# A two-layer graph network: the nodes between the layers as a pipeline of chunks, with shared message buffers

## The chip, the cores and the metric

The kernel runs on one core of a Trainium2 chip. The core has five engines, each with an instruction queue of its own that is worked off in order: TensorE (PE in the profile; its weight loads are listed apart as PEld), VectorE (DVE), ScalarE (ACT), GpSimd (POOL) and SyncE (SP), which here only starts DMA transfers. Engines wait for each other by semaphores. The metric is the time of one execution on the device in microseconds. The tables quote single records of a profiled execution, which is one more execution beside the timed ones.

## What is computed

There are 6250 nodes with 64 features and 206,250 edges, sorted by destination. Each of two layers normalizes the nodes, sends a message along every edge, sums the messages at their destinations, and adds an update to the nodes. Cut to what matters:

```
h  = relu(layernorm(x))                       # over the 64 features
m  = segment_sum(relu(h[src] + ea16 @ We.T + be), dst)
g  = batchnorm((h + m) @ W1.T + b1)           # over the nodes
x  = x + relu(g) @ W2.T + b2                  # end of layer 0
h  = relu(layernorm(x))
y  = relu(concat(h[src], ea64) @ Mw.T + Mb)
z  = segment_sum(y, dst)
x  = x + relu(concat(h, z) @ Uw.T + Ub)       # end of layer 1
```

The change concerns the two lines in the middle: from `relu(g)` to the normalized `h` of layer 1 and to `h @ Mw_h.T + Mb`, the part of the message that depends on the source node alone, which the kernel keeps as a table with one row per node.

## The kernel before

Nodes lie in 49 tiles of 128, and the middle part works on chunks of 8 tiles: six full ones and one of a single tile. Edges come in groups of 16 x 128.

Edges are summed in two ways. The first 71 groups are sorted on the chip. For each group VectorE works out a place for every edge (`rank`), PE and ScalarE make the edge's row (`rows`), and GpSimd writes the rows to memory with 16 indirect DMAs (`scatter`, L605). A block of sorted rows then belongs to one tile of 128 destinations. There are 35 such blocks, of seven chunks each (`chunk`): a one-hot matrix of sources picks rows of the table by matmul (`gp`, L319), the message is finished (L324, or L326 and L327), a one-hot matrix of destinations is built (`hot_d`, L329), and a matmul sums the messages into `pa` (L333). The loading of a block (`eb`) and the preparation of its columns run ahead of it (`prepare`, `sources`).

The last 30 groups are not sorted. GpSimd fetches their rows of the table with 16 indirect DMAs per group (`gather`, L384) into `gat`, which has four buffers. `direct` then handles a group in two halves of 8 x 128 edges: the part from the edge features on PE (L402), its sum with the gathered rows on VectorE (L406), the relu on ScalarE (L407), a one-hot matrix on VectorE (L410) and the matmul into `pd` (L415), which is added to `acc` (L417). In the kernel before, `direct` has message and one-hot buffers of its own, `msg_d` and `hot_g`, two of each.

`unsorted` ties the two ways together in each layer. It issues the gathers of a group, lets the sorted stream advance by 4 steps (layer 0) or 8 (layer 1), a step being a chunk, and then calls `direct` for the group of three turns earlier.

After layer 0's sums come, on VectorE and PE, a few operations that find out whether any edge was left over (L727 to L733, the result is `any_i`); `general` loops over such edges, zero times for these inputs, and the engines load its number of rounds from `any_i`. Then batch norm is finished from statistics per tile (L757 to L768) and applied with a relu in seven parts of 896 columns (L771).

The middle is the loop from L780 on. For each chunk: product with W2 (`py`, L784); x loaded and b2 added (L786, L787); the sum (L788), stored as x1 (L789) for the end of layer 1; `norm_relu`, which is mean, centering, square, variance, root, reciprocal and the scaled maximum (L217 to L228); `transposed` in two halves through one PSUM bank (L240, L241); the product with the message weight (`pt`, L795); the bias (L797); the store of the table (L799); and `split` (L249 to L252), which keeps the table on the chip as three bf16 parts for the one-hot matmuls of layer 1. GpSimd's gathers of layer 1 wait until the table is stored.

The order in each queue comes from a scheduler that takes the program's order and the buffers of its pools into account: an instruction that writes a buffer waits until the readers of its former contents are done. Only where the program asks for it is an order kept as written.

Of the kernel before, what the change touches and what calls it, by code (L numbers as in the profile page):

```python
# [49 lines left out]
NB = 49  # L50
NP = P * NB
# [44 lines left out]
def gnn_kernel(  # L96
# [22 lines left out]
    nc = tc.nc  # L119

    const = ctx.enter_context(tc.tile_pool(name="const", bufs=1))
# [5 lines left out]
    def bank(shape, name, tag, bufs=1, dtype=F32):  # L127
        return ps.tile(shape, dtype, name=name, tag=tag, bufs=bufs)
# [103 lines left out]
    def by_node(t):  # L232
        return t[:, :NP].rearrange("c (j p) -> c j p", j=NB)
# [162 lines left out]
    def direct(layer, g, gat, ea, to, pool):  # L396

        pd = bank([P, P], "pd", "rk")
        for a in range(0, GT, 8):
            pm = bank([P, 8, D], "pm_d", "pm", 2)  # L400
            if layer == 0:
                nc.tensor.matmul(pm, ea[:, a // 8, :], we0, start=True, stop=True)  # L402
# [3 lines left out]
            nc.vector.tensor_add(msg, pm, gat[:, a:a + 8, :])  # L406
# [76 lines left out]
    with tc.tile_pool(name="sort", bufs=1) as sort:  # L483
# [177 lines left out]
        for j0, j1 in chunks:  # L661
            n = j1 - j0
# [27 lines left out]
    for g in range(GS, NG):  # L690
# [4 lines left out]
    nc.vector.scalar_tensor_tensor(marked[:, GS * GT:], dst_d, float(PAD), wide,  # L695
                                   op0=OP.is_lt, op1=OP.mult)

    def unsorted(layer, table, steps, per_group, window_of, done):
# [28 lines left out]
    most = ln.tile([P, 1], F32, name="most")  # L727
    nc.vector.tensor_reduce(most, marked, AX.X, OP.max)
    p = bank([P, P], "most_p", "tr")
    nc.tensor.transpose(p, most.to_broadcast([P, P]), ident)  # L730
    any_f = ln.tile([1, 1], F32, name="any_f")
    nc.vector.tensor_reduce(any_f, p[0:1, :], AX.X, OP.max)
    nc.vector.tensor_scalar(any_i, any_f, float(NB), None, op0=OP.mult)  # L733

    w2_sb = weight(w2_t, "w2_sb")
    mx_sb = weight(mw_t[0:D, :], "mx_sb")
    uh_sb = weight(uw_t[0:D, :], "uh_sb")
    uz_sb = stacked(uw_t[D:2 * D, :], "uz_sb")
    b2_b = spread(b2, "b2_b")
    mb_b = spread(mb, "mb_b")  # L740
    ub_b = spread(ub, "ub_b")
    gamma_c = column(gamma, "gamma_c")
    beta_c = column(beta, "beta_c")
# [32 lines left out]
    late = ctx.enter_context(tc.tile_pool(name="late", bufs=1))  # L776
    h1t = late.tile([D, NP], F32, name="h1t")
    x1 = dram.tile([NP, D], F32, name="x1")
    x1_rows = x1.rearrange("(j p) d -> p j d", p=P)
    for j0, j1 in chunks:  # L780
        n = j1 - j0
        py = bank([P, 8, D], "py", "gp", 2)
        for j in range(j0, j1):
            nc.tensor.matmul(py[:, j - j0, :], by_node(acc)[:D, j, :], w2_sb, start=True, stop=True)  # L784
        xs = ln.tile([P, 8, D], F32, name="xc", bufs=2)[:, :n, :]
        nc.sync.dma_start(xs, x_rows[:, j0:j1, :])  # L786
        nc.vector.tensor_add(xs, xs, b2_b[:, None, :].to_broadcast([P, n, D]))  # L787
        nc.vector.tensor_add(xs, xs, py[:, :n, :])  # L788
        nc.sync.dma_start(x1_rows[:, j0:j1, :], xs)  # L789
        h = ln.tile([P, 8, D], F32, name="h", bufs=2)  # L790
        norm_relu(h, xs)
        transposed(h1t, h, j0, j1)
        pt = bank([P, 8, D], "pt", "gp", 2)
        for j in range(j0, j1):
            nc.tensor.matmul(pt[:, j - j0, :], by_node(h1t)[:, j, :], mx_sb, start=True, stop=True)  # L795
        tabf = ln.tile([P, 8, D], F32, name="tabf", bufs=2)
        nc.vector.tensor_add(tabf[:, :n, :], pt[:, :n, :],  # L797
                             mb_b[:, None, :].to_broadcast([P, n, D]))
        nc.sync.dma_start(table1_rows[:, j0:j1, :], tabf[:, :n, :])  # L799
        split(tabf, j0, j1)  # L800


    def output(h_t, z_t, x_b, to, pool):
# [97 lines left out]
```

## Time and profile before

| What | us |
|---|---|
| Median of three runs (lowest, highest) | 3044.73 (3044.18, 3052.03) |
| The profiled execution, and its span | 4316.56, 4314.7 |
| PE busy, PEld busy, DVE, ACT, POOL (whole span) | 2107.8, 1511.2, 1591.5, 622.3, 2089.7 |
| Last scatter, first gather of layer 0 | 2117.4, 2120.91 |
| Batch norm finished (start of the first relu, L771) | 2990.65 |
| First product of the middle (L784) | 2991.84 |
| First message of layer 1 (L326), first gather of layer 1 | 3088.90, 3089.98 |
| One scatter, one gather (L605, L384), mean | 1.035, 0.944 |

How to read it: each engine's busy time is an average over stages that have different limits, so the stages are read one by one. A line of the timeline or of the groups has the start, the duration, the engine, the source line, the operation with its output and inputs, the shape, and in brackets how long the engine had been idle before it and what released it. "Issue" and "remote" name idle time for which the profile shows no releaser on this core. The profiled execution is 1.42 times as long as the median.

### The profile page before, as it was taken

What the parts mean: (1) busy time and instruction counts of PE and PEld (TensorE: products, weight loads), DVE (VectorE), ACT (ScalarE), POOL (GpSimd) and SP (SyncE); (2) the same over time, 40 slices, a digit from 0 to 9 for tenths busy, and PEclk for the clock granted to TensorE, in tenths of its full rate; (3) what the DMA queues carried; (4) which work ended last, traced back from release to release, by engine and by line L of the source; (5) the groups of instructions that cost most, each with busy time, mean ns of one, the idle gap of its engine ahead of it and who ended that gap; (6) DMA issues with size and microseconds to landing.
All of it is one profiled execution on the core that took longest, in us unless ns stands there. A gap on an engine that the chain in (4) does not pass through costs nothing.

```text
span 4314.7 us, 58769 instructions
## 1 busy us (share of the span) xinstructions
PE 2107.8 (49%) x22799; PEld 1511.2 (35%) x22799; DVE 1591.5 (37%) x3467; ACT 622.3 (14%) x1313; POOL 2089.7 (48%) x2106
## 2 busy tenths in 40 slices
PE   3344554544455544545335332234456665566666
PEld 2233332333333323333123111113444454445545
DVE  7333443443344333434113111113244453444445
ACT  2111111111111111111011000001111111111111
POOL 6556555555655555565642665552233433443341
PEclk6666766766677667667568555555577776777777
DMA  8564655645555555655232111112144443444442
GB/s 204 147 186 158 185 146 155 192 144 171 180 169 169 156 137 155 188 178 146 75 121 79 28 28 25 25 26 72 43 145 137 142 145 127 134 139 131 160 136 80
DMA packets 310816, 556.78 MB, mean 129 GB/s; under 512 B 100484, under 2 KB 174468, under 8 KB 301572
## 3 DMA queue, kind: packets, MB, share of 16 engines
q1 hardware_dynamic: 231744, 470.66, 35.6%
q0 software_dynamic: 67072, 79.29, 7.3%
q10 hardware_dynamic: 11716, 3.03, 0.4%
q8 instruction: 181, 2.97, 0.3%
q14 instruction: 103, 0.84, 0.1%
HBM read 367.38 MB, written 185.38 MB: 128 GB/s over the span
## 4 chain that ended last, share of the span: by engine, by line
PE 35%; another core or an unknown queue 32%; issue 18%; DMA 6%; DVE 4%; ACT 3%; POOL 1%; SPq 0%; DVEq 0%; ACTq 0%; POOLq 0%
PE pa L333 11%; PE gp L319 8%; PE gp L267 5%; DMA eb<-place 3%; PE pm L258 3%; PE pd L415 3%; DMA gat<-table,src_d 1%; PE pm_d L258 1%; PE pm_d L402 1%; DVE msg L326 1%; ACT msg L324 1%; DMA xc<-in_x 1%; POOL gat L384 1%; PE at_p L265 1%
## 5 line engine op out<-in xcount | busy, mean ns | idle before, releaser
L605 POOL DMA_INDIRECT place<-to,ix x1136 | 1175.7, 1035 | 935.6 <-ACT at L266 467.6
L384 POOL DMA_INDIRECT gat<-table,src_d x960 | 906.0, 944 | 1077.3 <-DVE msg_d L406 759.6
L333 PE MATMUL pa<-hot_d,msg 128*64 128x128 f32 x7000 | 623.7, 316 | 794.6 <-issue 419.3
L333 PEld LDWEIGHTS pa<-hot_d,msg 128*64 128x64 f32 x7000 | 467.2, 157 | 999.4 <-issue 490.9
L329 DVE TENSOR_TENSOR hot_d<-cbank,dl 128x1024 f32<-128x1024 f32 (+1 forms) x490 | 539.4, 1104 | 693.9 <-remote 405.2
L319 PE MATMUL gp<-tab,hot_s 128*128 128x64 bf16 x5250 | 263.2, 209 | 276.7 <-issue 239.4
L319 PE MATMUL gp<-tab,st 128*128 128x64 bf16 x5250 | 259.6, 203 | 248.8 <-issue 160.1
L267 PE MATMUL gp<-we,at 128*128 128x512 f32 (+1 forms) x490 | 306.2, 709 | 89.2 <-issue 59.6
L324 ACT ACTIVATE msg<-gp 128x512 f32<-128x512 f32 (+1 forms) x245 | 135.1, 551 | 1408.6 <-remote 854.9
L319 PEld LDWEIGHTS <-hot_s 128*128 128x128 bf16 x5250 | 215.8, 108 | 340.9 <-issue 296.5
L310 DVE TENSOR_SCALAR hot_s<-st,pcol 128x1024 bf16<-128x1024 bf16 (+1 forms) x245 | 111.9, 461 | 579.1 <-remote 444.3
L319 PEld LDWEIGHTS <-st 128*128 128x128 bf16 x5250 | 214.4, 105 | 307.2 <-issue 301.3
L326 DVE TENSOR_TENSOR msg<-gp,eb 128x512 f32<-128x512 f32 (+1 forms) x245 | 152.2, 628 | 370.5 <-remote 253.3
L327 ACT ACTIVATE msg<-msg 128x512 f32<-128x512 f32 (+1 forms) x245 | 142.4, 584 | 881.2 <-DVE msg L326 729.5
L415 PE MATMUL pd<-hot_g,msg_d 128*64 128x128 f32 x1920 | 199.5, 348 | 121.9 <-DVE acc L417 68.1
L402 PE MATMUL pm_d<-we,ea_d 128*128 128x512 f32 x120 | 104.1, 965 | 273.6 <-DVE msg_d L406 174.0
L415 PEld LDWEIGHTS pd<-hot_g,msg_d 128*64 128x64 f32 x1920 | 152.0, 177 | 210.4 <-issue 189.2
L258 PE MATMUL pm<-we,ea 128*128 128x128 f32 x1136 | 193.4, 314 | 66.0 <-DMA ea<-in_ea 25.5
L417 DVE TENSOR_TENSOR acc<-acc,pd 128x128 f32<-128x128 f32 x60 | 17.2, 287 | 494.7 <-remote 387.0
L258 PEld LDWEIGHTS pm<-we,ea 128*128 128x128 f32 x1136 | 165.1, 218 | 90.2 <-issue 60.8
L410 DVE TENSOR_TENSOR hot_g<-cbank,rel_d 128x1024 f32<-128x1024 f32 x120 | 145.3, 1216 | 116.4 <-remote 65.2
L407 ACT ACTIVATE msg_d<-msg_d 128x512 f32<-128x512 f32 x120 | 75.4, 629 | 524.2 <-DVE msg_d L406 381.5
(133 smaller groups left out, 1843.2 us busy)
## 6 DMA issues: line engine op xcount, KB each, us to landing
eb<-place SPq DMA_DIRECT2D x70, 2050.0 KB
place<-minus SPq DMA_DIRECT2D x35, 2050.0 KB
st<-src_rows SPq DMA_DIRECT2D x210, 256.0 KB
hots<-hot_s SPq DMA_DIRECT2D x210, 256.0 KB
st<-hots SPq DMA_DIRECT2D x210, 256.0 KB
ea<-in_ea SPq DMA_DIRECT2D x71, 512.0 KB
place<-to,ix POOLq DMA_INDIRECT x1136
gat<-table,src_d POOLq DMA_INDIRECT x960
```

The source lines that it names most:

```text
L258: nc.tensor.matmul(half_tiles[:, 2 * k:2 * k + 2, :], ea[:, k, :], we1, start=True, stop=True)
L267: nc.tensor.matmul(gp[:, :n, :], at[:n * ED, :], we0[:n * ED, :n, :], start=True, stop=stop)
L319: nc.tensor.matmul(gp[:, t, :], hot_s[:, t, :], tab[:, sb, k, :], start=(layer == 1 and k == 0), stop=(k == 2 and (layer == 1 or t == n - 1)))
L324: nc.scalar.activation(msg[:, :n, :], gp[:, :n, :], AF.Relu)
L326: nc.vector.tensor_add(msg[:, :n, :], gp[:, :n, :], eb[:, a:b, 0:D])
L329: nc.vector.tensor_tensor(hot_d[:, :n, :], slot_p[:, None, :].to_broadcast([P, n, P]), dl[:, a:b, :].to_broadcast([P, n, P]), op=OP.is_equal)
L333: nc.tensor.matmul(pa[at:at + D, :], msg[:, t, :], hot_d[:, t, :], start=(a + t < 2), stop=(a + t >= T - 2))
L384: nc.gpsimd.indirect_dma_start(out=gat[:, t, :], out_offset=None, in_=table, in_offset=bass.IndirectOffsetOnAxis(ap=src_d[:, k:k + 1], axi ...
L402: nc.tensor.matmul(pm, ea[:, a // 8, :], we0, start=True, stop=True)
L410: nc.vector.tensor_tensor(hot, slot_p[:, None, :].to_broadcast([P, 8, P]), rel_d[:, k:k + 8, None].to_broadcast([P, 8, P]), op=OP.is_equal)
L415: nc.tensor.matmul(pd[at:at + D, :], msg[:, t, :], hot[:, t, :], start=(a + t < 2), stop=(a + t >= GT - 2))
L605: i = nc.gpsimd.indirect_dma_start(out=place[:, :], out_offset=bass.IndirectOffsetOnAxis(ap=ix[:, t:t + 1], axis=0), in_=to[:, t, :], in_o ...
```

## The change

Four things change.

1. `direct` takes its two buffers from the same rings as the sorted chunks (`msg` and `hot_d`, two buffers each) instead of having `msg_d` and `hot_g`.
2. The operations that make `any_i` and the loads of the later weights move from behind layer 0's gathers to ahead of them. So does a new preparation: `xc`, which is x + b2 with its mean over the features taken away, for all nodes; and `w2cw`, a pair of weights: W2 with the mean of its columns taken away, and W2 itself.
3. In the middle, a chunk is multiplied with both weights. Since the mean over features is linear, the product with the centered weight plus `xc` is already the centered node (`cen`), without a mean to be found first. The plain node (product with W2 itself, plus x + b2) is needed for the end of layer 1 alone; ScalarE copies the product out of PSUM and GpSimd adds it.
4. The chunks run as a pipeline that is written out: each turn issues the stages of several chunks (relu of the next, linear of this one, normalization of the one before, the message product of the one before that, and so on), and PE, VectorE and ScalarE keep this order.

```diff
             else:
                 edge_terms_1(pm, ea[:, a // 2:a // 2 + 4, :])
-            msg = pool.tile([P, 8, D], F32, name="msg_d", bufs=2)
+            msg = work.tile([P, 8, D], F32, name="msg")
             nc.vector.tensor_add(msg, pm, gat[:, a:a + 8, :])
             nc.scalar.activation(msg, msg, AF.Relu)
-            hot = pool.tile([P, 8, P], F32, name="hot_g", bufs=2)
+            hot = work.tile([P, 8, P], F32, name="hot_d")
...
+    most = ln.tile([P, 1], F32, name="most")
...
+    nc.vector.tensor_scalar(any_i, any_f, float(NB), None, op0=OP.mult)
...
+    w2cw = const.tile([D, 2, D], F32, name="w2cw")
+    nc.scalar.dma_start(w2cw[:, 1, :], w2_t)
+    w2m = ln.tile([D, 1], F32, name="w2m")
+    nc.vector.tensor_reduce(w2m, w2cw[:, 1, :], AX.X, OP.add)
+    nc.vector.tensor_scalar_mul(w2m, w2m, 1.0 / D)
+    nc.vector.tensor_scalar(w2cw[:, 0, :], w2cw[:, 1, :], w2m, None, op0=OP.subtract)
+    late = ctx.enter_context(tc.tile_pool(name="late", bufs=1))
+    mid_stack = ExitStack()
+    mid = mid_stack.enter_context(tc.tile_pool(name="mid", bufs=1))
+    xc = mid.tile([P, NB, D], F32, name="xc")
+    for j0, j1 in chunks:
+        n = j1 - j0
+        nc.sync.dma_start(xc[:, j0:j1, :], x_rows[:, j0:j1, :])
+        nc.vector.tensor_add(xc[:, j0:j1, :], xc[:, j0:j1, :], b2_b[:, None, :].to_broadcast([P, n, D]))
+        mean = ln.tile([P, 8, 1], F32, name="mean")
+        nc.vector.tensor_reduce(mean[:, :n, 0], xc[:, j0:j1, :], AX.X, OP.add)
+        nc.vector.tensor_scalar_mul(mean[:, :n, :], mean[:, :n, :], 1.0 / D)
+        nc.vector.tensor_sub(xc[:, j0:j1, :], xc[:, j0:j1, :], mean[:, :n, :].to_broadcast([P, n, D]))
...
-    for a in range(0, NP, NP // 7):
-        b = a + NP // 7
-        nc.scalar.activation(acc[:D, a:b], acc[:D, a:b], AF.Relu, bias=bn_shift, scale=bn_scale)
...
-    for j0, j1 in chunks:
-        n = j1 - j0
-        py = bank([P, 8, D], "py", "gp", 2)
...
+    class Nodes:
...
+        def relu(self):
+            t = acc[:D, self.j0 * P:self.j1 * P]
+            nc.scalar.activation(t, t, AF.Relu, bias=bn_shift, scale=bn_scale)
+
+        def linear(self):
+            self.pc = bank([P, 8, D], "pc", "gp", 2)
+            self.py = bank([P, 8, D], "py", "pm", 2)
+            for k, to in enumerate((self.pc, self.py)):
+                for j in range(self.j0, self.j1):
+                    nc.tensor.matmul(to[:, j - self.j0, :], by_node(acc)[:D, j, :], w2cw[:, k, :],
+                                     start=True, stop=True)
+
+        def centered(self):
+            n = self.n
+            self.cen = mid_2.tile([P, 8, D], F32, name="cen", bufs=2)[:, :n, :]
+            nc.vector.tensor_add(self.cen, self.pc[:, :n, :], xc[:, self.j, :])
+            self.sq = ln.tile([P, 8, D], F32, name="sq")[:, :n, :]
+            nc.scalar.activation(self.sq, self.cen, AF.Square)
+            xs = ln.tile([P, 8, D], F32, name="xc", bufs=2)[:, :n, :]
+            nc.sync.dma_start(xs, x_rows[:, self.j, :])
+            nc.gpsimd.tensor_add(xs, xs, b2_b[:, None, :].to_broadcast([P, n, D]))
+            y = mid_2.tile([P, 8, D], F32, name="y", bufs=2)[:, :n, :]
+            nc.scalar.copy(y, self.py[:, :n, :])
+            nc.gpsimd.tensor_add(xs, xs, y)
+            nc.sync.dma_start(x1_rows[:, self.j, :], xs)
+
+        def variance(self):
+            self.var = mid_2.tile([P, 8, 1], F32, name="var", bufs=2)[:, :self.n, :]
+            nc.vector.tensor_reduce(self.var[:, :, 0], self.sq, AX.X, OP.add)
+            nc.scalar.activation(self.var, self.var, AF.Sqrt, bias=eps, scale=1.0 / D)
+
+        def norm(self):
+            n = self.n
+            rstd = ln.tile([P, 8, 1], F32, name="rstd")
+            nc.vector.reciprocal(rstd[:, :n, :], self.var)
+            h = ln.tile([P, 8, D], F32, name="h", bufs=2)
+            nc.vector.scalar_tensor_tensor(h[:, :n, :], self.cen, 0.0,
+                                           rstd[:, :n, :].to_broadcast([P, n, D]),
+                                           op0=OP.max, op1=OP.mult)
+            transposed(h1t, h, self.j0, self.j1)
+
+        def product(self):
+            self.pt = bank([P, 8, D], "pt", ("pa", "rk")[self.c % 2])
+            for j in range(self.j0, self.j1):
+                nc.tensor.matmul(self.pt[:, j - self.j0, :], by_node(h1t)[:, j, :], mx_sb,
+                                 start=True, stop=True)
...
+    step = ((-1, Nodes.relu), (2, Nodes.product), (3, Nodes.second), (0, Nodes.linear),
+            (2, Nodes.table), (1, Nodes.variance), (3, Nodes.third), (0, Nodes.centered), (1, Nodes.norm))
+    with tc.manual_schedule(engines={mybir.EngineType.PE, mybir.EngineType.DVE,
+                                     mybir.EngineType.Activation}):
+        for k in range(-1, len(nodes) + 3):
+            for far, stage in step:
+                if 0 <= k - far < len(nodes):
+                    stage(nodes[k - far])
```

`table`, `second` and `third`, left out here, are the bias with the store of the table, and the two halves of `split`. GpSimd's adds and the DMAs of SP are not among the engines whose order is kept: the scheduler places them. In the changed kernel two of GpSimd's adds of b2 (L826) come to stand among the scatters of layer 0, behind the 48th and the 112th, because they need nothing but x and b2.

More of the change, by code (lines that the diff above doesn't have):

```diff
@@ L696, in gnn_kernel @@
                                    op0=OP.is_lt, op1=OP.mult)
+    most = ln.tile([P, 1], F32, name="most")
+    nc.vector.tensor_reduce(most, marked, AX.X, OP.max)
+    p = bank([P, P], "most_p", "tr")
+    nc.tensor.transpose(p, most.to_broadcast([P, P]), ident)
+    any_f = ln.tile([1, 1], F32, name="any_f")
+    nc.vector.tensor_reduce(any_f, p[0:1, :], AX.X, OP.max)
+    nc.vector.tensor_scalar(any_i, any_f, float(NB), None, op0=OP.mult)
+    mx_sb = weight(mw_t[0:D, :], "mx_sb")
+    uh_sb = weight(uw_t[0:D, :], "uh_sb")
+    uz_sb = stacked(uw_t[D:2 * D, :], "uz_sb")
+    b2_b = spread(b2, "b2_b")
+    mb_b = spread(mb, "mb_b")
+    ub_b = spread(ub, "ub_b")
+    gamma_c = column(gamma, "gamma_c")
+    beta_c = column(beta, "beta_c")
+    w2cw = const.tile([D, 2, D], F32, name="w2cw")
[16 more added lines that the diff above has]
+        nc.vector.tensor_sub(xc[:, j0:j1, :], xc[:, j0:j1, :], mean[:, :n, :].to_broadcast([P, n, D]))
     def unsorted(layer, table, steps, per_group, window_of, done):
@@ L724, in gnn_kernel @@
              lambda d: finish_0(d, None))
[L727 to L743, printed above, removed]
     def more_0(b, delta, pool):
@@ L768, in gnn_kernel @@
     nc.vector.tensor_sub(bn_shift, beta_c, bn_shift)
-    for a in range(0, NP, NP // 7):
-        b = a + NP // 7
-        nc.scalar.activation(acc[:D, a:b], acc[:D, a:b], AF.Relu, bias=bn_shift, scale=bn_scale)
     table1 = dram.tile([NP, D], F32, name="table1")
     table1_rows = table1.rearrange("(j p) d -> p j d", p=P)
-    late = ctx.enter_context(tc.tile_pool(name="late", bufs=1))
     h1t = late.tile([D, NP], F32, name="h1t")
@@ L779, in gnn_kernel, with __init__, table, second @@
     x1_rows = x1.rearrange("(j p) d -> p j d", p=P)
-    for j0, j1 in chunks:
-        n = j1 - j0
-        py = bank([P, 8, D], "py", "gp", 2)
[L783 to L800, printed above, removed]
+    class Nodes:
+        def __init__(self, c):
+            self.c = c
+            self.j0, self.j1 = chunks[c]
+            self.n = self.j1 - self.j0
+            self.j = slice(self.j0, self.j1)
+        def relu(self):
[39 more added lines that the diff above has]
+                                 start=True, stop=True)
+        def table(self):
+            n = self.n
+            self.tabf = ln.tile([P, 8, D], F32, name="tabf", bufs=2)[:, :n, :]
+            nc.vector.tensor_add(self.tabf, self.pt[:, :n, :], mb_b[:, None, :].to_broadcast([P, n, D]))
+            nc.sync.dma_start(table1_rows[:, self.j, :], self.tabf)
+            nc.scalar.copy(tab[:, self.j, 0, :], self.tabf)
+        def second(self):
+            nc.vector.tensor_sub(self.tabf, self.tabf, tab[:, self.j, 0, :])
+            nc.scalar.copy(tab[:, self.j, 1, :], self.tabf)
+        def third(self):
+            nc.vector.tensor_sub(tab[:, self.j, 2, :], self.tabf, tab[:, self.j, 1, :])
@@ new lines, in gnn_kernel @@
+    mid_2 = mid_stack.enter_context(tc.tile_pool(name="mid_2", bufs=1))
+    nodes = [Nodes(c) for c in range(len(chunks))]
+    step = ((-1, Nodes.relu), (2, Nodes.product), (3, Nodes.second), (0, Nodes.linear),
[6 more added lines that the diff above has]
+                    stage(nodes[k - far])
@@ L803, in output @@
+    mid_stack.close()
     def output(h_t, z_t, x_b, to, pool):
```

## The prediction

> **What bounds the kernel now.** I read the page first. Its span is 4314.7 us, and the profiled execution took 4316.56 us, so 1.9 us lie around the span. The median of the runs shown is 3044.73 us, 0.71 of that. The chain of the page says where the excess sits: 32% of it is "another core or an unknown queue" and 18% "issue".
>
> ```profile
> PE 35%; another core or an unknown queue 32%; issue 18%; DMA 6%; DVE 4%; ACT 3%; POOL 1%; SPq 0%; DVEq 0%; ACTq 0%; POOLq 0%
> ```
>
> Those stretches, in which TensorE gets an instruction only every microsecond or two, lie in the scatter stage, at its end and in layer 1. So the profiled execution can't be scaled as a whole. I work out differences inside stretches that run evenly, in microseconds of the profile, and set them against the median unscaled, because an even stretch should last as long in every execution. This kernel's measurement can tell about 0.3%, 9.1 us.
>
> Second, the table of windows over the middle, 2992 to 3083 us (columns: window, length, busy time of PE, PEld, DVE, ACT, POOL, clock, DMA share, GB/s):
>
> ```profile
> 2992.00:3083.00 91.00, 55.70 (x246) 48.84 (x246) 36.07 (x65) 24.61 (x40) 0.00 (x0) 0.50 0.25 65
> ```
>
> PE is busy for 61% and GpSimd not at all, so each chunk of 8 tiles is a chain with idle PE in it. Third, the timeline shows that chain:
>
> ```profile
> 3025.65 0.69 DVE L788 TENSOR_TENSOR xc<-xc,py 128x512 f32<-128x512 f32 x1 [2.72 <-PE py L784]
> ...
> 3030.18 0.69 DVE L228 SCALAR_TENSOR_TENSOR h<-cen,rstd 128x512 f32<-128x512 f32 x1
> ...
> 3031.02 1.03 PE L240 MATMUL ht_p<-ident,h 128*64 128x128 f32 x4 [5.40 <-DVE h L228]
> ...
> 3033.71 3.68 PE L795 MATMUL pt<-mx_sb,h1t 64*128 64x64 f32 x16
> ...
> 3037.18 3.62 PE L784 MATMUL py<-w_sb,acc 64*128 64x64 f32 x16
> ```
>
> The vector chain from L788 to L228 keeps PE waiting 5.40 us in each chunk. L784 follows from 3022.00 to 3037.18, a period of 15.18 us. Fourth, the waits of GpSimd after the scatters (columns: waiter, releaser, total, times, longest), and its first two:
>
> ```profile
> POOL gat L384 <- DVE msg_d L406: 195.4, 13, 76.3
> POOL gat L384 <- issue: 139.7, 451, 2.5
> ```
> ```profile
> 2227.31 0.69 DVE L406 TENSOR_TENSOR msg_d<-pm_d,gat 128x512 f32<-128x512 f32 x1 [1.53 <-PE pm_d L402]
> ...
> 2230.87 0.94 POOL L384 DMA_INDIRECT gat<-table,src_d  x1 [30.32 <-DVE acc L630]
> ```
>
> Gathers run at 0.94 + 0.30 us each, and a group of 16 at 19.97 us. Four groups fit; the fifth waits for the first `direct` (L406). After that GpSimd sets the pace of the remaining groups, so how many are left when the buffers start to come free matters.
>
> [...] PE is full from 3003.34 to 3010.4 us, yet the clock stays at 0.50. [...]
>
> **The change, part by part.**
>
> *Middle.* Before: the first L784 starts at 2991.84, the first message of layer 1 (L326) at 3088.90, 97.1 us later. After: each chunk does three products, 3 x 3.47 us in a dense stream (the spacing of L795 and L784 above: 3.37 to 3.47), and the transposes, 2.72 us from the first to the product (3030.99 to 3033.71), because both halves share one PSUM bank and its copy. That is 13.13 us of PE. VectorE has six operations of 0.69 us and a reciprocal of 0.20, 4.3 us; ScalarE's relu of 1.25, square, copy of y and two casts at 0.62, a square root of 0.30 and two copies of 0.58 make 5.2[...]. Their cover is PE, and h of the chunk before is ready inside the 3.7 us of the second product: after the last pass of pc come 0.69 + 0.63 + 0.69 + 0.30 + 0.20 + 0.69 = 3.2 us, and a wait of a whole step lies between. Without that cover the 5.4 us return. Six chunks: 78.8 us; the last, of one tile, 2.6; two chunks of layer 1 put in between (45 matmuls), 2.7; the tail of the last table and the first message, 1.2. Sum 85.3 us, and 0.1 for the first relu, now of 1024 columns. The gain is 97.1 - 85.4 = **11.7**. The gathers of layer 1, which wait for the table, start earlier too.
>
> *any_i.* L727 to L733 move ahead of the gathers. Between the last L417, which ends at 2982.48, and the batch norm at 2987.77 now lie most_p, any_f, any_i and 3.13 us of idle time, in which engines load the number of blocks. With the value long there: 2982.48 + 3.13 = 2985.6, **-2.1**.
>
> *Weights, xc precomputed.* 7 chunks x (3 x 0.69 + 0.17) make up to 16 us of VectorE and 7 more loads on SP, all ahead of the sorted tail's end. VectorE waits there for rows of the last blocks (2 to 9 us each in the waits of VectorE), which hides about half; the eb load of the last block but one goes behind a store of hot_s in SP's order, 3 to 5 us.
>
> *GpSimd's adds.* Two L826 stand between scatters #48/#49 and #112/#113. [...] nothing if the queue waits for rows there anyway, which it does in the profile at #113. I take **+1.3** (0 to 2.6). What queues behind are scatters, and behind them the sorted blocks. The other adds run while GpSimd would be idle.
>
> *Shared buffers, layer 0.* `msg_d` and `hot_g` go; `direct` now takes its buffers in turn with the sorted chunks. In VectorE's order before, the first L406 stands three blocks ahead of the sorted end, in the changed kernel only behind the last block. Let T be the end of the last scatter; a sorted block takes about 27 us. Before: VectorE stops for the first gathered group (T + 27), three blocks follow, T + 108, the next `direct` 6 us later: T + 114, with 25 groups to gather, 499 us: T + 613. After: no stop; the last two blocks begin after the rows (9 us) and their preparation (12), T + 21 + 54 + about 20 for xc and the late eb = T + 95, + 6, but 26 groups, 519: T + 620. **+7**, from -11 (gathering resumes the moment the four groups are done, T + 83 + 519) to +20 (the sorted end doesn't move).
>
> *Shared buffers, layer 1.* PE is busy there for 31.6 of 35 us between directs, gathers take 20.0 us per group, and 8 chunks with a direct take 19.7 us of PE: balanced. Directs now stand in fixed places (chunks 32, 32, 40, 40 against 25, 27, 34, 39), and wait for the chunks' buffers. I take **+4** (0 to 30) and give back **-2** for the two products already done.
>
> Sum: -11.7 - 2.1 + 1.3 + 7 + 4 - 2 = -3.5. Against the profiled 4316.56 that is 4313.1; against the median, 3044.73 - 3.5, **3041 us**.
>
> **Rivals.** (A) *The buffers cost nothing*: if the handover is 0 or below and layer 1 absorbs the new order, -11.7 - 2.1 + 1.3 - 2 = -14.5 is left, and up to 11 more: 3019 to 3034, middle 3030. For: VectorE loses the 24 us stop. Against: one group more is still to gather. (B) *The clock warms*: [...] as windows of layer 1 do (0.88 at 2231 to 2327). Warm, 64-row loads of the same kind (L805, L806) take 186 ns in the trace, cold 330; a chunk falls to 8 or 9 us and the gain to 35 to 45: 3005. Against: the 0.50 over full windows. (C) *Layer 1 turns into the loss*: a direct half takes a `msg` and a `hot` buffer from the chunk stream, and PE waits for ScalarE's L327 (0.33 to 0.77 us in the waits of PE). At 60 halves x 0.6 = 36 us instead of 4 the sum is +28: 3073; at 0.4, +17: 3062. It decides from about 0.22 us a half (13 us, sum +6) and shows as slower from 0.3 (18 us). For: two buffers for both. Against: many such waits are hidden behind gathers. (D) *xc is not hidden, or the early weights wait*: that is the end +20 of layer 0: 3054. (E) *The pipeline doesn't run as written*, one of its buffers making the chunks follow one another again: the middle gives nothing, -3.5 + 11.7 = +8 to +12: 3055.
>
> **How the numbers follow.** Forecast, the small balance: 0.36; A 0.22; B 0.12; C 0.18; D 0.10; E 0.02. Its own range is 3030 to 3052. For 8 in 10 I cut half of B below (0.06) and the top of C above (0.10): **3003 to 3066**. Faster by over 0.3% (below 3035.6): A (0.22), B (0.12), and 0.10 of the forecast: 0.44. Within 0.3% (to 3053.8): 0.26 of the forecast and a third of D: 0.29. Slower: C, the rest of D, and E: 0.27.
>
> **What would show it.** In the middle: L784's counterpart every 13 us, the transposes waiting for nothing but PE, [...] first message some 85 us after the first product. If the period is 15 or more, the pipeline waits for a buffer; at 9, B. In layer 0: GpSimd has four groups, not five, before the sorted end, and 26 after. In layer 1: PE's waits for `msg` and `hot_d` between chunks. The forecast is wrong if the sorted end moves by more than 15 us, if the order in layer 1 costs 20, or if GpSimd's adds take several microseconds.

## The result: 0.6% slower

The changed kernel takes 3064.02 us (median of seven runs, 3060.94 to 3071.07), the kernel before 3044.73 us (seven runs, 3037.21 to 3052.03). The ratio is 1.006, with a 95% interval of 1.0045 to 1.0076. So it is slower by 19 us, where the forecast said 3 or 4 us faster, too little to be measured.

One and the same kernel takes 3045 to 3090 us on some chips and 4300 to 4420 us on others (the profile of before that the prediction read was one of the latter), so a ratio is taken only between kernels that ran on one chip, and stage lengths are compared only within one of the two groups, called "3050 chips" and "4300 chips" here. Ratios are worked out from the single runs and can differ a little from the ratio of the two medians.

### The profile after

Its profiled execution took 3063.92 us, the span is 3062.1 us, and PE is busy for 62% of it. The part that was rewritten does what it says. The table of windows over the middle (window, length, busy time of PE, PEld, DVE, ACT, POOL, clock, DMA share, GB/s):

```profile
2276.00:2350.00 74.00, 70.44 (x319) 64.81 (x320) 19.06 (x34) 25.32 (x43) 12.80 (x12) 0.50 0.23 51
```

PE is busy for 95% (70.44 of 74.00 us), where it was 61%; VectorE and ScalarE are hidden under it. The timeline of one chunk of the changed kernel:

```profile
2309.40 3.62 PE L815 MATMUL pc<-w2cw,acc 64*128 64x64 f32 x16
...
2312.81 3.62 PE L815 MATMUL py<-w2cw,acc 64*128 64x64 f32 x16
...
2316.36 1.06 PE L240 MATMUL ht_p<-ident,h 128*64 128x128 f32 x4
...
2317.25 1.26 POOL L829 TENSOR_TENSOR xc<-xc,y 128x512 f32<-128x512 f32 x1 [10.67 <-ACT y L828]
...
2319.08 3.67 PE L850 MATMUL pt<-mx_sb,h1t 64*128 64x64 f32 x16
...
2322.55 3.62 PE L815 MATMUL pc<-w2cw,acc 64*128 64x64 f32 x16
```

From one product with `pc` to the next is 13.15 us (2309.40 to 2322.55), against 15.18 before. The first transposes of a chunk have no idle time ahead of them any more. GpSimd's add takes 1.26 us and no engine waits for it here.

The loss is elsewhere. Around the last scatter the timeline of the changed kernel shows this:

```profile
1586.50 0.28 DVE L310 TENSOR_SCALAR hot_s<-st,pcol 128x256 bf16<-128x256 bf16 x1
...
1636.11 0.38 SPq L731 DMA_DIRECT2D xc<-in_x  x1
...
1639.12 0.69 DVE L732 TENSOR_TENSOR xc<-xc,b_b 128x512 f32<-128x512 f32 x1 [52.34 <-DMA xc<-in_x]
...
1641.81 1.98 PE L333 MATMUL pa<-hot_d,msg 128*64 128x128 f32 x16 [50.04 <-DVE hot_d L329]
```

VectorE reaches L732, the first operation of the new preparation, and stands there for 52.34 us. Its load of x (L731) starts only at 1636.11, 1.4 us after the last scatter has ended (1634.7). Behind L732 in VectorE's order wait the one-hot matrices of the sorted block, and PE waits 50 us for them. SP's own waits name the scatters' DMAs, in the changed kernel (first line) for the load of `xc` and in the kernel before (second line, run `e13_before_sixth`) for the load of `direct`'s edge features (`ea_d`):

```profile
SPq L731 <- DMA place<-to,ix: 52.3, 4, 48.5
```
```profile
SPq L392 <- DMA place<-to,ix: 49.7, 4, 46.0
```

Neither load reads what the scatters write. Both go into pools that are opened after the pool of the scatter stage has been closed, so the likely reason is that they get its memory; no run tests this.

The 52 us are not the loss, though. VectorE stands about as long around the last scatter in the kernel before (`e13_before_sixth`), for the first gathered group:

```profile
1679.64 0.69 DVE L406 TENSOR_TENSOR msg_d<-pm_d,gat 128x512 f32<-128x512 f32 x1 [57.61 <-DMA gat<-table,src_d]
```

With shared buffers alone it stands for 49.87 us (`e18_shared_fourth`). What differs is what follows. In the changed kernel the load of the last sorted block but one starts 31.6 us after the last scatter, behind loads of x and behind stores that wait for VectorE, and PE stops for it. With shared buffers alone it is one of two loads that start right after the last scatter (1669.28 in that run). The changed kernel:

```profile
1666.28 0.37 SPq L368 DMA_DIRECT2D eb<-place  x1
...
1676.71 0.42 PE L277 MATMUL st_p<-ident,eb 128*50 128x128 f32 x1 [4.89 <-DMA eb<-place]
```

and `e18_shared_fourth`:

```profile
1672.99 0.91 SPq L368 DMA_DIRECT2D eb<-place  x2
```

What the changed order does to the gathers is seen in GpSimd's waits between the last scatter and the end of layer 0 (waiter, releaser, total us, times, longest). The changed kernel:

```profile
POOL gat L384 <- issue: 140.6, 454, 2.5
POOL gat L384 <- DVE msg L406: 21.9, 1, 21.9
```

and the kernel before, in its one profile from a 3050 chip (`e13_before_sixth`, span 3077.0 us):

```profile
POOL gat L384 <- issue: 142.7, 461, 2.5
POOL gat L384 <- DVE msg_d L406: 12.2, 1, 12.2
```

Each has one stop. In the kernel before it comes after five groups, in the changed one after four, and is longer. From the end of the last scatter, the group behind the stop starts after 115.0 us before (25 groups are left) and after 107.6 us in the changed kernel (26 left); the last gather ends after 614.0 and 626.9 us.

Another loss is at the entry of layer 1. Timeline of the changed kernel:

```profile
2357.81 0.37 SPq L857 DMA_DIRECT2D table<-tabf  x1
...
2358.23 0.57 SPq L368 DMA_DIRECT2D eb<-place  x1
...
2366.30 0.21 DVE L282 TENSOR_SCALAR dl<-eb 128x50 f32<-128x50 f32 x1 [3.64 <-DMA eb<-place]
2366.42 0.69 DVE L326 TENSOR_TENSOR msg<-gp,eb 128x512 f32<-128x512 f32 x1
```

and of the kernel before (`e13_before_sixth`):

```profile
2288.08 0.34 SPq L368 DMA_DIRECT2D eb<-place  x1
...
2292.61 3.67 PE L784 MATMUL py<-w_sb,acc 64*128 64x64 f32 x16 [7.69 <-ACT acc L771]
```

Before, the loads of layer 1's first two blocks stood ahead of the middle; the line shows the second (L368), 4.5 us ahead of the first product. In the changed kernel both stand among the last stores of the middle in SP's order (the second at 2361.81), and the first message waits: VectorE had nothing else to do for 3.64 us when the block came.

The stages on 3050 chips, in us. "Tail" is from the end of the last scatter to the last L417, "middle" from the first product to the first L326, "layer 1" from there to the last addition to the output (L887, which is L809 in the kernel before); another 10 to 12 us follow to the end of the span.

| kernel | tail | to batch norm (bn_aggr) | to first product | middle | layer 1 | sum |
|---|---|---|---|---|---|---|
| before (`e13_before_sixth`) | 621.5 | 5.6 | 3.8 | 97.1 | 675.6 | 1403.6 |
| changed | 634.8 | 2.8 | 3.9 | 90.2 | 684.2 | 1415.9 |
| buffers shared, else as before (`e18_shared_fourth`) | 625.8 | 6.7 | 4.4 | 97.0 | 683.3 | 1417.2 |
| changed, own buffers in layer 1, xc in the gathers (`e14_own1_xc_in_gathers`) | 625.7 | 2.8 | 3.9 | 92.8 | 683.0 | 1408.2 |
| changed, own buffers in both, early load (`e17_own_both_third`) | 621.0 | 3.3 | 3.9 | 75.1 | 694.0 | 1397.3 |

The stages behind the scatters account for +12.3 of the 19.3 us. Where the other 7 us lie is not shown: the only profile of before from a 3050 chip is from another chip, where its runs have a median of 3067.84 us, and the stretch up to the last scatter can't be compared (1661.7 us there, 1634.7 in the changed kernel). The lengths behind the scatters carry over better, as far as is seen: the last row, which has the buffers of the kernel before in the tail, is from yet another chip and has a tail of 621.0 us (621.5 before). Two adds came to stand among the scatters; they last 3.0 us together, and what they cost was not measured by itself. Timeline of the changed kernel:

```profile
100.17 1.74 POOL L826 TENSOR_TENSOR xc<-xc,b_b 128x512 f32<-128x512 f32 x1
...
191.86 1.29 POOL L826 TENSOR_TENSOR xc<-xc,b_b 128x512 f32<-128x512 f32 x1
```

### The profile page after: what moved, and what is told of

Same layout as the page of the kernel before. It is cut to its first block, busy times and chain, and to the rows that moved or that the text cites. A ratio compares the mean times of both kernels' runs of the same rounds, so it can differ in the third digit from the quotient of the medians.

```text
span 3062.1 us, 59128 instructions
## 1 busy us (share of the span) xinstructions
PE 1891.5 (62%) x22897; PEld 1409.3 (46%) x22897; DVE 1589.8 (52%) x3470; ACT 628.0 (21%) x1320; POOL 2133.9 (70%) x2120
## 5 line engine op out<-in xcount | busy, mean ns | idle before, releaser
L333 PE MATMUL pa<-hot_d,msg 128*64 128x128 f32 x7000 | 523.1, 293 | 99.4 <-DVE hot_d L329 52.3
L329 DVE TENSOR_TENSOR hot_d<-cbank,dl 128x1024 f32<-128x1024 f32 (+1 forms) x490 | 538.8, 1101 | 65.9 <-PE pa L333 62.2
L333 PEld LDWEIGHTS pa<-hot_d,msg 128*64 128x64 f32 x7000 | 406.0, 145 | 242.7 <-ACT msg L324 134.1
L319 PE MATMUL gp<-tab,hot_s 128*128 128x64 bf16 x5250 | 229.3, 206 | 406.8 <-DVE hot_s L310 399.9
L282 DVE TENSOR_SCALAR dl<-eb 128x50 f32<-128x50 f32 x70 | 16.0, 229 | 507.7 <-DMA eb<-place 506.1
L267 PE MATMUL gp<-we,at 128*128 128x512 f32 (+1 forms) x490 | 264.3, 622 | 10.7 <-ACT at L266 10.5
L319 PE MATMUL gp<-tab,st 128*128 128x64 bf16 x5250 | 213.3, 196 | 79.9 <-DVE msg L326 60.4
L406 DVE TENSOR_TENSOR msg<-pm_d,gat 128x512 f32<-128x512 f32 x120 | 82.6, 688 | 242.1 <-DMA gat<-table,src_d 225.6
L410 DVE TENSOR_TENSOR hot_d<-cbank,rel_d 128x1024 f32<-128x1024 f32 x120 | 145.9, 1216 | 88.7 <-PE pd L415 86.3
L415 PEld LDWEIGHTS pd<-hot_d,msg 128*64 128x64 f32 x1920 | 139.0, 173 | 101.4 <-issue 76.0
L415 PE MATMUL pd<-hot_d,msg 128*64 128x128 f32 x1920 | 173.8, 338 | 19.1 <-ACT msg L407 15.7
L407 ACT ACTIVATE msg<-msg 128x512 f32<-128x512 f32 x120 | 75.6, 630 | 500.6 <-DVE msg L406 499.0
```

The source lines that it names most:

```text
L267: nc.tensor.matmul(gp[:, :n, :], at[:n * ED, :], we0[:n * ED, :n, :], start=True, stop=stop)
L319: nc.tensor.matmul(gp[:, t, :], hot_s[:, t, :], tab[:, sb, k, :], start=(layer == 1 and k == 0), stop=(k == 2 and (layer == 1 or t == n - 1)))
L329: nc.vector.tensor_tensor(hot_d[:, :n, :], slot_p[:, None, :].to_broadcast([P, n, P]), dl[:, a:b, :].to_broadcast([P, n, P]), op=OP.is_equal)
L333: nc.tensor.matmul(pa[at:at + D, :], msg[:, t, :], hot_d[:, t, :], start=(a + t < 2), stop=(a + t >= T - 2))
```

## The experiments

Two theories stood at the start. S: the stop at L732 delays the sorted tail and with it the gathers. B: the buffers that `direct` now shares with the sorted chunks cost the time in layer 1. Most runs came to 4300 chips. There PE stands idle in layer 1 for reasons that the profile doesn't show ("issue"), and the effects are larger. The kernel before on a 4300 chip (`e6_before_third`):

```profile
PE gp L319 <- issue: 144.8, 171, 2.6
PE pa L333 <- issue: 126.5, 125, 3.8
```

and on a 3050 chip (`e13_before_sixth`), where L333 has no such wait:

```profile
PE gp L319 <- issue: 1.0, 2, 0.7
```

The stages on 4300 chips, in us, columns as above:

| run | tail | to bn_aggr | middle | layer 1 | ratio to before (95% interval) |
|---|---|---|---|---|---|
| before, `e1_before_again` | 868.2 | 5.6 | 97.0 | 1214.6 | |
| before, `e6_before_third` | 859.9 | 5.5 | 97.1 | 1214.4 | |
| changed, `e7_after_again` | 885.3 | 2.8 | 89.9 | 1251.7 | 1.013 (1.0105 to 1.0156) |
| shared only, `e2_shared_only` | 872.1 | 6.7 | 97.1 | 1250.1 | 1.0103 (1.0068 to 1.0137) |
| own in layer 1, `e3_own_layer1` | 885.5 | 2.8 | 92.4 | 1214.8 | 1.0024 (0.9999 to 1.0049) |
| xc in gathers, `e4_xc_in_gathers` | 865.5 | 2.9 | 92.7 | 1250.5 | 1.0081 (1.0053 to 1.0108) |
| own in both, `e5_own_both` | 866.9 | 3.4 | 75.1 | 1224.8 | 0.9971 (0.9952 to 0.999) |

`e8_shared_look` and `e16_shared_third` repeat the shared buffers (the first with 1253.4 us in layer 1, the second with a ratio of 1.0109, 1.0086 to 1.0133), and `e15_own_both_again` the version with own buffers (1223.2 us, ratio 0.9987, 0.9969 to 1.0006).

### The kernel before and the changed kernel again

Nothing is edited. The first was

> The kernel before, unchanged, for a second profile of it, since the first was 1.42 times as long as its runs. Measured so far: 3044.7 us before, 3064.0 after, so +19.3; the middle of the changed kernel is some 9 us shorter, so other stages must have lost about 28 us. Theory S (the stop): in the changed kernel VectorE stops 52.3 us at L732, whose load of x waits for the end of the scatters, and the sorted tail behind it ends late; then the kernel before should take from the end of the last scatter to the last L417 some 607 to 615 us, against 634.8 after, and the same in layer 1 (695.7 us from the first L326 to the end, within 8). Theory B (shared buffers in layer 1): layer 1 of the kernel before should take about 668 us, and layer 0's tail the same 630 to 638.

It came out at 4328.21 us and showed that the profile of before wasn't a single disturbed one. Only `e13_before_sixth` met a 3050 chip (3078.79 us; 3067.84 the median of the kernel before on that chip):

> The kernel before, for its stages beside the next kernel's. If of 4300 to 4400 us: tail 860 to 875, first L784 to first L326 97.1, from there 1214 to 1223. If of 3040: layer 1 650 to 672 us (the changed kernel 684.2), tail 612 to 628 (changed 634.8).

Its tail of 621.5 us is where it was expected, 13.3 us below that of the changed kernel. Its layer 1, 675.6 us, is above what was expected: 8.6 us less than in the changed kernel, not 12 or more. The changed kernel on a 4300 chip:

> The changed kernel, unaltered, beside its variants. Theory B with S as the smaller part: on a chip that takes 4320 us for the kernel before, layer 1 takes 1250 us from the first L326 on (1214 before), the tail of layer 0 885 us (865 before), the middle 92.5, so +44 to +50 us, a ratio of 1.010 to 1.012. On a chip that takes 3045, 1.006 again.

4371.08 against 4308.8 us, ratio 1.013, just above what was expected. The stages move as expected: +21 in the tail (against the mean of the two profiles of before in the table), +37 in layer 1, -7 in the middle, -3 at batch norm.

### Shared buffers alone

```diff
-            msg = pool.tile([P, 8, D], F32, name="msg_d", bufs=2)
+            msg = work.tile([P, 8, D], F32, name="msg")
...
-            hot = pool.tile([P, 8, P], F32, name="hot_g", bufs=2)
+            hot = work.tile([P, 8, P], F32, name="hot_d")
```

On a 4300 chip:

> The kernel before with part 1 of the change alone: direct takes its buffers from the rings msg and hot_d, in both layers; any_i, the weights, the middle as before, no xc. VectorE's order has the first direct behind the last block, as after, and layer 1's directs at chunks 32, 32, 40, 40. Theory S: nothing stops VectorE before the end of the scatters, the loss is small or none: 3033 to 3048. Theory B: nearly the whole loss is here: 3062 to 3075.

Layer 1 grew from 1214.6 to 1250.1 us; the tail by 4 us, within what profiles of before differ by. What was expected of this run, and of the next two versions, is given in times of a 3050 chip; on a 4300 chip it can only be read for its direction. On a 3050 chip:

> Shared buffers alone, on the kernel before, for a chip of some 3050 us; at 4300 its ratios were 1.010 and 1.011. At 3050: tail some 625 us from the last scatter to the last L417 (621.5 before). If sharing costs nothing in layer 1 there, 675 to 681 us from the first L326 (675.6 before) and a ratio of 1.001 to 1.003; if it costs, above 690 and a ratio above 1.006. At 4300 again: 1250 to 1254 against 1214, 1.010.

3099.24 against 3088.73 us, ratio 1.0042 (1.0026 to 1.0057), some 13 us. The stages say where: tail +4.3, layer 1 +7.7, batch norm and first product +1.7. So sharing costs in both layers, in layer 1 far less than on a 4300 chip (7.7 against 35.5 us); the result lies between the two cases of the expectation. GpSimd's waits in layer 1 of this run:

```profile
POOL gat L384 <- DVE dl L282: 27.4, 3, 11.1
POOL gat L384 <- DVE msg L406: 20.4, 11, 3.7
```

and of `e13_before_sixth`:

```profile
POOL gat L384 <- DVE msg_d L406: 37.4, 10, 11.6
```

GpSimd waits for `direct` more evenly, but longer in all (48 against 37 us), and some of the waits now end behind the preparation of a sorted block (L282).

### Own buffers in layer 1 alone

```diff
-            msg = work.tile([P, 8, D], F32, name="msg")
+            if layer == 1:
+                msg = pool.tile([P, 8, D], F32, name="msg_d", bufs=2)
+            else:
+                msg = work.tile([P, 8, D], F32, name="msg")
```

and the same for the one-hot matrix. The other parts of the change stay.

> The changed kernel, but in layer 1 alone direct has msg_d and hot_g of its own again (the room of xc is free by then); VectorE's order in layer 1 is then that of the kernel before (chunks 26, 27, 34, 40). Theory S: layer 1 is not where it is lost: 3055 to 3067. Theory B: the loss goes: 3034 to 3042.

Layer 1 is back at 1214.8 us, and the ratio falls to 1.0024. On 4300 chips B is shown for layer 1. The tail stays long (885.5 us): that part isn't in layer 1.

### xc made during the gathers

```diff
+        i = nc.sync.dma_start(xc[:, j0:j1, :], x_rows[:, j0:j1, :])
+        tc.add_manual_dep(i.ins, after.ins.name, SYNC, reason="behind a group of the gathers")
...
+                if layer == 0 and 0 <= c - GS - 14 < len(chunks):
+                    centered_x(c - GS - 14, added)
```

> The changed kernel, but xc is made during layer 0's gathers, one chunk behind each of seven groups (the 15th to the 21st), by a wait of its load on that group's L417; the buffers stay shared. VectorE's order then has no L732 before the last block. Theory S: the 52 us stop is gone, the sorted tail ends earlier, and gathers begin again close to 83 us after the last scatter: 3030 to 3046. Theory B: 3060 to 3066, as after.

The tail falls from 885.3 to 865.5 us; the middle is 2.8 us longer, and the ratio stays high for layer 1's sake (1250.5 us). So the preparation of xc costs in the tail and the shared buffers in layer 1: both theories named a right place, each for a part of the loss. But this edit takes the stop away together with the loads and the work of xc, so it doesn't show that the stop itself is what costs. Both edits together met a 3050 chip:

> The changed kernel with both causes taken out in the least way: direct has its own buffers in layer 1, and xc is made during the gathers of layer 0; in layer 0 the buffers stay shared. The sum of stages gives tail 865 us, middle 92, layer 1 as in the kernel before: 5 to 10 us off the kernel before, ratio 0.997 to 0.9995. If sharing in layer 0 costs by itself (the order of the first direct), the tail is 873 to 880 and the ratio 1.000 to 1.002.

3072.15 against 3067.84 us, ratio 1.0014 (0.9998 to 1.003). GpSimd's stop of the tail:

```profile
POOL gat L384 <- DVE msg L409: 14.2, 1, 14.2
```

(L409 of that file is L406 of the changed kernel.) With xc out of the way the tail is 625.7 us: of the 13.3 us that the changed kernel loses there, 9.1 go with xc, and 4.2 with the sharing, as in `e18_shared_fourth` (4.3). That is the expectation's second case. How the sorted blocks end on 3050 chips, in us after the last scatter:

| kernel | load of the last block but one (L368) starts | last one-hot matrix of the sorted blocks (L329) | first gather behind GpSimd's stop | groups left |
|---|---|---|---|---|
| before (`e13_before_sixth`) | 3.8 | 108.1 | 115.0 | 25 |
| buffers shared (`e18_shared_fourth`) | 4.3 | 99.8 | 99.1 | 26 |
| changed, own buffers in layer 1, xc in the gathers (`e14_own1_xc_in_gathers`) | 3.8 | 97.9 | 97.1 | 26 |
| changed | 31.6 | 108.3 | 107.6 | 26 |

VectorE stops for 50 to 58 us around the last scatter in all four. The late load is found in the changed kernel alone, and so is the later end, 8.5 us behind that of shared buffers alone. So the record speaks for the load that stands behind xc, and against the length of the stop; a run that changes the load alone was not made.

The sum of stages is not below that of before. The first message comes 4.3 us earlier than before, and layer 1 takes 7.4 us more, although its buffers are its own: the gain of the middle doesn't last to the end. Against the changed kernel, own buffers give back only 1.2 us in layer 1 here (683.0 against 684.2). So on 3050 chips B is not shown for the changed kernel, although sharing alone cost 7.7. One wait is longer in all three kernels that lose there: VectorE's wait for the loads of sorted blocks, here of before (`e13_before_sixth`) and of the changed kernel:

```profile
DVE dl L282 <- DMA eb<-place: 69.4, 24, 12.6
```
```profile
DVE dl L282 <- DMA eb<-place: 76.0, 25, 14.4
```

It is 75.2 us in `e18_shared_fourth` and 79.6 in `e14_own1_xc_in_gathers`. Whether it is the cause was not tested.

### What layer 1 loses by

In layer 1 of the changed kernel both halves of a `direct` stand together in VectorE's order. Setting them apart by four chunks keeps the rings:

```diff
+            if a == 0:
+                between()
...
-            for _ in range(per_group):
+            for _ in range(per_group // 2 if apart else per_group):
```

> The changed kernel, buffers shared as in it, but in layer 1 the two halves of direct are set apart by four chunks of the sorted stream (VectorE's order: directs at chunks 28, 32, 36, 40 in place of 32, 32, 40, 40). If what costs the time in layer 1 is that both halves stand together in the stream (order), layer 1 falls from 1250 us to 1214 to 1225, and the ratio to the kernel before from 1.013 to 1.003 to 1.006. If it is the rings of two buffers themselves (buffers), layer 1 stays at 1243 to 1256 and the ratio at 1.011 to 1.015. The tail of layer 0 (885) and the middle (90 to 92.5) stay. On a chip of 3040: order, layer 1 shorter than 684 by 8 us or more.

Layer 1 took 1237.9 us, against 1221.4 in the profile of before from that chip (`e10_before_fourth`): +16.5 in place of +37. The ratio was 1.007 (1.0048 to 1.0092). Neither case: the place in the order is about half of it. Deeper rings:

```diff
-        msg = work.tile([P, 8, D], F32, name="msg")
+        msg = work.tile([P, 8, D], F32, name="msg", bufs=3)
...
-        hot_d = work.tile([P, 8, P], F32, name="hot_d")
+        hot_d = work.tile([P, 8, P], F32, name="hot_d", bufs=3)
```

and the same in `direct`.

> The changed kernel with three buffers instead of two in the shared rings msg and hot_d (room from the rows of the scatter stage, ea with two buffers for three, so the time up to the last scatter is not compared). The order of layer 1 stays that of the changed kernel: directs at chunks 32, 32, 40, 40. If the rings' depth is what is left of the loss in layer 1 (halves apart got back about 20 of 37 us): layer 1 from 1250 to 1214 to 1235. If the place in the order is all of it: 1245 to 1256. On a chip of 3040: below 676, or 680 to 686.

1269.8 us, with 1223.1 in the kernel before on that chip (`e11_before_fifth`): +47. In these two single profiles a third buffer gave nothing back. What the other half of the loss on 4300 chips is stays open.

### A version that beats both

Own buffers in both layers; no `xc` ahead of the middle: x is centered chunk by chunk in the pipeline, so that its memory isn't needed while the gathers run; the first block of layer 1 is loaded ahead of the middle, and the second can follow.

```diff
+        def centered_x(self):
...
+            nc.vector.tensor_reduce(mean[:, :n, 0], self.xs, AX.X, OP.add)
+            nc.vector.tensor_scalar_mul(mean[:, :n, :], mean[:, :n, :], 1.0 / D)
...
+            nc.vector.tensor_sub(self.xc, self.xs, mean[:, :n, :].to_broadcast([P, n, D]))
...
+    first = load_block(0)[0]
...
-    steps = blocks(1, lambda d: load_block(d)[0], lambda d: True, finish_1)
+    steps = blocks(1, lambda d: load_block(d)[0] if d else first, lambda d: True, finish_1)
```

> The changed kernel with what the theories name taken out: direct has msg_d and hot_g of its own in both layers, xc is not made ahead but chunk by chunk inside the pipeline (VectorE then has 6.5 us of work per chunk, under PE's 13.1), and the first block of layer 1 is loaded before the middle. Orders of layer 0's tail and of layer 1 are then those of the kernel before. B and S: only the middle's gain is left, 7 to 14 us off the kernel before, of which 2 to 3 at any_i: 3030 to 3038, or a ratio of 0.9965 to 0.998 where the kernel before takes 4320. If something else in the change costs time, 1.000 or above.

4298.12 against 4308.8 us, 0.9971 (0.9952 to 0.999), as expected; the repeat on another chip gave 0.9987 (0.9969 to 1.0006), which can't be told from no change. On a 3050 chip:

> The version with own buffers in both layers, x centered inside the pipeline and the first block of layer 1 loaded ahead, a third time, for a chip of some 3050 us; at 4300 its two ratios were 0.997 and 0.999, with middle and layer 1 together 1298 to 1300 us against 1311.5. At 3050: if the early load keeps the middle's gain, middle and layer 1 take 760 to 766 us against 772.7 before (775.8 with the load behind the middle), ratio 0.995 to 0.998; if layer 1 gives it back anyway, 770 to 776 and 0.998 to 1.001.

3078.17 against 3088.73 us, ratio 0.9962 (0.9949 to 0.9976), about 12 us off. Timeline of this run:

```profile
2302.21 0.34 SPq L368 DMA_DIRECT2D eb<-place  x1
...
2318.68 0.15 DVE L282 TENSOR_SCALAR dl<-eb 128x50 f32<-128x50 f32 x1
...
2382.56 0.69 DVE L326 TENSOR_TENSOR msg<-gp,eb 128x512 f32<-128x512 f32 x1
```

The second block's load starts 5.2 us ahead of the first product (2307.42), and the first message comes after 75.1 us, in the middle itself. Middle and layer 1 together take 769.1 us, against 772.7 before and 775.8 with the load behind the middle; on 4300 chips 1299.9 against 1311.5 and 1307.2. The ratio is in the first case of the expectation, but the 769.1 us lie between its two cases: of the middle's gain only 3.6 us are left at the end. The period of the chunks is 13.15 us as in the changed kernel, so VectorE's added work is hidden. That the early load makes the difference of some 7 us to the load behind the middle is what the lines suggest; it was not undone by itself, so it isn't shown alone.

## Why the prediction was wrong

Three terms of the sum failed, by 5 to 7 us each: the end of the middle, where a load was put at nothing, the handover in layer 0, and layer 1. The measured 3064.02 us lie inside the range of 3003 to 3066, near its upper end, but the change went the other way. Term by term, on 3050 chips:

- *Middle, -11.7.* The mechanism was right: dense products, a period of 13.13 us forecast, 13.15 measured, everything else hidden. The end was not: the first message came after 90.2 us, not 85.4. The lines show why: the load of the first block (L368) stands at the middle's end in SP's order, and what waits for it begins at 2366.30. The step "the tail of the last table and the first message, 1.2" left out that DMA. -6.9 in place of -11.7.
- *any_i, -2.1.* Measured -2.8 to batch norm. Right.
- *GpSimd's adds, +1.3.* 1.74 and 1.29 us among the scatters, 1.26 elsewhere (128x512, L826 and L829 of the changed kernel). The term was the author's estimate: the profile of before has no add on GpSimd to measure. The two among the scatters last 3.0 us together, more than the term and small; what they cost in the end is not known.
- *Weights and xc, and shared buffers in layer 0, +7 (-11 to +20).* With T for the end of the last scatter: the model gave T + 114 for the sixth group and T + 613 for the last gather of the kernel before, and the profile shows 115.0 and 614.0. For the changed kernel it gave T + 101 and T + 620; measured 107.6 and 626.9. The tail grew by 13.3, not 7. That it came so near is luck, for two errors work against each other in it. The step that failed is "the last two blocks begin after the rows": without a stop for the first gathered group, one block fewer was to be left behind T. Three blocks are loaded behind T in the shared kernels as in the kernel before, and with no xc at all the sorted end (the last L329) is at T + 99.8 (`e18_shared_fourth`) where the model's sum without xc is T + 75. Against that, 20 us were set for xc and the late eb, and xc moved the sorted end by only 8.5 us, to T + 108.3. The late load of the last block but one was named in the prediction, with 3 to 5 us; it starts some 27 us later than with shared buffers alone.
- *Layer 1, +4 - 2.* Measured +8.6. Sharing alone costs 7.7 (`e18_shared_fourth`), but with own buffers (`e14_own1_xc_in_gathers`) layer 1 was nearly as long. Of the two products done ahead nothing is to be seen. The size failed; the cause on 3050 chips stays open.

Rival D named the tail's end, "the sorted end doesn't move", and priced it at +20: the sorted end was indeed at T + 108.3 against 108.1 before. It cost 13.3, because the gathers went on at T + 107.6, just ahead of that end and not 6 us behind it. Rival C named layer 1 as the loss: there it is, but at some 8 us on 3050 chips and 37 on 4300 chips. C's mechanism, rings of two buffers that run dry, is not shown: on 4300 chips own buffers gave the time back (1214.8 us), but a ring of three gave nothing, and on a 3050 chip own buffers gave back 1.2 us. The measured time came from both together, each smaller than it was priced, a case that the list did not have. B (the clock) did not come: 0.50 over 74 us of a PE that is 95% busy. That it would rise in this stage was the author's assumption, which the profile doesn't show. The prediction's window for B (0.88 at 2231 to 2327) is also misread: it lies at the sorted end of layer 0, not in layer 1, where the same profile has 0.76 (3190 to 4314).

How the reading went wrong: the forecast took lengths from a profile in which the excess over the runs lay in the very stages, tail and layer 1, that decided the sign. That it couldn't be scaled was said; that costs there were known less well than the middle's was not drawn into the chances.

## What to carry to other kernels

Work that is moved ahead "into idle time" of an in-order engine brings its own waits with it: before it is called hidden, ask when its earliest input can start, and what is queued behind that input. Here the loads of x started only 1.4 us after the last scatter, VectorE stood 52.34 us at the first operation that needs them (L732), and a block's load that stood behind them came 27 us later. A long stop that is new in a profile is not yet the loss: look whether the engine stood as long at that place before (here 52.34 us and, before, 57.61). A stage that is made shorter can lose its gain where the next stage's first loads are issued later than before; here they came behind the middle's stores, and VectorE had nothing else to do for 3.64 us ahead of the first message.

## What was not expected of the hardware

- The same kernel takes 3045 to 3090 us on some chips and 4300 to 4420 on others. In the kernel before, the last scatter is done after 1661.7 us on the one kind (`e13_before_sixth`) and after 2118.4 and 2125.7 on the other (the profile of before that the prediction read, and `e1_before_again`), and layer 1 takes 675.6 and 1214 to 1223 us, while the middle takes 97.1 on both. In layer 1 the mean granted clock is 0.94 on the one (`e13_before_sixth`) and 0.74 on the other (3088.9 to 4314.7 us of the profile that the prediction read). A change's ratio differs too: 1.0042 and 1.010 for shared buffers alone. Only one chip was met twice (4300 us both times), so chip and occasion are hardly told apart, and the reason stays open.
- TensorE's granted clock stayed at 0.50 through the 74 us of the dense middle, with PE busy for 70.44 of them.
